# Convolution weights' zeros and bands issued by SyncE instead of GpSimd

## The chip, the cores and the metric

The kernel runs on one core of one Trainium2 chip. The metric is the device time of one execution in microseconds (us); the kernel before has a median of 3051.75 us over three runs (3051.0 to 3055.79). The core has five engines that run side by side, each through its own list of instructions: TensorE (PE, matrix products), VectorE (DVE), ScalarE (ACT), GpSimd (POOL) and SyncE (SP). SP, ACT and POOL issue DMA transfers. All transfers run on the same 16 DMA engines of the core, but each issuing engine has its own queue there.

## The reference

Two layers work on an image x of shape (2, 256, 64, 64) in float32. The first is attention over all 4096 pixels of an image with 8 heads, mixed with x by a mask. The second is a channel gate, attention in windows of 8 x 8 pixels, and two grouped 7 x 7 convolutions (64 groups of 4 channels), whose result gates x.

```python
# layer 0
m = jax.image.resize(mask, (B, 1, H, W), method='bilinear')
q, k, v = proj(Wq, bq) / math.sqrt(hd), proj(Wk, bk), proj(Wv, bv)
attn = jax.nn.softmax(jnp.einsum('bnd,bmd->bnm', q, k), axis=-1)
fuse = jnp.einsum('bnm,bmd->bnd', attn, v)
hybrid = _conv1x1(jnp.concatenate([x, fuse], axis=1), Wf, bf)
x = hybrid * m + x * (1.0 - m)
# layer 1
x = x * sigmoid(relu(xp @ ca_w1 + ca_b1) @ ca_w2 + ca_b2)
x = x + window_attention(x) @ out_w + out_b
x = channel_shuffle(x, 4)
y = lax.conv_general_dilated(x, sa_w1, (1, 1), [(3, 3), (3, 3)], feature_group_count=cr)
y = relu(_bn(y + sa_b1))
y = lax.conv_general_dilated(y, sa_w2, (1, 1), [(3, 3), (3, 3)], feature_group_count=cr)
y = _bn(y + sa_b2)
return x * jax.nn.sigmoid(y)
```

## The kernel before

A first part (to about 187 us) projects x to q, k and v and stores them to scratch tensors in HBM. Beside it, `prepare` (L166) builds from the convolutions' parameters two small tables `r1_s` and `r2_s` and a block of zeros `zero_s`, all in HBM; its DMAs go through POOL, ending with L303, L324 and L327. The stores of v (L484) go through POOL too.

`pipeline` (L523) does the attention of the first layer in 1024 slots. A slot is one image, one chunk of 512 queries, one group of four heads and one block of 128 keys. PE computes the scores (L632) two slots ahead, ACT the exponentials (L642) into one of eight buffers e, PE the products with v (L661), and DVE adds the exponentials up for the denominators (L663). Every four slots need one piece of k and one of v, 256 KB each. `load_piece` (L552) issues both on SP two pieces ahead; there are three buffers for each, so a load waits until PE is through with the piece that lay in its buffer. SP also loads q (L566), x and the mask (L572, L575).

The rest of the two layers for a finished chunk (`stage`, L720) is mixed into later slots; it starts a few slots after the chunk's last one, so the first 64 slots and some more have none of it. At the end of a stage the chunk's result goes to the scratch `x_s` by DMAs on POOL (L978). Slots run in the order written here; nothing reorders the instructions of an engine.

The convolutions at the end (`convolve`, L991) read their weights as banded matrices from the scratch `w_s` (16 blocks, one for each `u`), with `load_w` (L1006, SP). `bands` (L337) writes these blocks. It is a generator that issues one DMA at each step: 16 copies of `zero_s` into the 16 blocks (L341, 896 KB each), and then 156 bands: 28 rows of `r1_s` (L349), 112 rows of `r2_s` (L355) and 16 shift rows (L362), each spread along a diagonal of all 16 blocks in pieces of 112 or 28 bytes. The loop over slots takes one step when the slot's number leaves 1 on division by five (L1188), and drains what is left before it starts the convolutions' first loads at slot 960 (L1170):

```python
            if i % 5 == 1:
                next(banded, None)
            if i % 4 == 0:
                run_stages()
```

A step puts the DMA into its engine's list at that place of the program. When it is issued depends on what that engine waits for. On POOL there is little else in these slots: the stores of `x_s` at the end of a stage, later a few stores of the output.

Of the kernel before, what the change touches and what calls it, by code (L numbers as in the profile page):

```python
# [55 lines left out]
def conv_seq_kernel(ctx: ExitStack, tc: tile.TileContext, a, out):  # L56
    nc = tc.nc
# [68 lines left out]
    w_s = dram.tile([NU, P, 2 * 32 * UW], F32, name="ws")  # L126
# [33 lines left out]
    zero_s = dram.tile([P, 2 * 32 * UW], F32, name="zeros")  # L160
# [171 lines left out]
    def spread(row, n):  # L332
        f = row.shape[-1]
        return row.rearrange("p u f -> u p f").to_broadcast([NU, n, f])


    def bands():  # L337
        band1 = w_s.rearrange("u p (m f) -> u (p m) f", f=UW)
        band2 = w_s.rearrange("u p (m f) -> u (p m) f", f=UW // 4)
        for u in range(NU):  # L340
            nc.gpsimd.dma_start(w_s[u], zero_s)  # L341
            yield
        for q in range(4):
            for dy in range(KS):
                r0, r1 = max(0, dy - PAD), min(RB, RB + dy - PAD)
                p0, m0, n = 32 * q + 1 + r0, 1 + r0 - dy + PAD, r1 - r0
                k = KS * q + dy
                at0, step = p0 * 64 + m0, 64 + 1
                nc.gpsimd.dma_start(  # L349
                    band1[:, at0 : at0 + step * (n - 1) + 1 : step, :], spread(r1_s[k : k + 1], n)  # L350
                )
                yield
                for i in range(4):
                    at0, step = p0 * 256 + 128 + i * 32 + m0, 256 + 1
                    nc.gpsimd.dma_start(  # L355
                        band2[:, at0 : at0 + step * (n - 1) + 1 : step, :],
                        spread(r2_s[k : k + 1, :, i], n),
                    )
                    yield
            for i in range(4):  # L360
                at0 = 32 * q * 256 + 128 + i * 32 + 1
                nc.gpsimd.dma_start(  # L362
                    band2[:, at0 : at0 + RB, :], spread(r2_s[32 + q : 33 + q, :, i], RB)
                )
                yield
# [157 lines left out]
    def pipeline(arm, shifted, pools):  # L523
# [628 lines left out]
        def run_stages():  # L1152
            while stages:
# [3 lines left out]
                stages.popleft()  # L1157

        banded = bands()

        nc.scalar.activation(warm, ones[0:1, 0:1], AF.Exp)
# [132 lines left out]
```

## Time and profile before

| what | us |
|---|---|
| median of three runs | 3051.75 |
| the profiled execution | 3062.01 |
| its span | 3060.2 |
| PE busy | 2967.3 |
| DVE busy | 2498.5 |
| ACT busy | 2478.7 |
| POOL busy | 369.4 |
| first scores of the attention start | 187.1 |
| last scores end, about | 2823 |

A busy time counts an engine's own work; the rest of the span it waits. What it waited for stands in brackets in the order of time and in the list of waits. The profile calls SP's issuing of DMAs SPq, and says for a group of DMAs on POOL how long they took from issue to landing. In names such as `ka<-ks` the target stands first: `ka` is the piece of k in the core's memory, `ks` its scratch in HBM, `ws` the weights' scratch, `zeros`, `r1s` and `r2s` what it is filled from.

### The profile page before, as it was taken

Reading aid. Unit: us, or ns where it says so; the run is one execution under the profiler, and the core shown is the slowest. Engines: PE = TensorE matmul, PEld = TensorE weight load, DVE = VectorE, ACT = ScalarE, POOL = GpSimd, SP = SyncE. Lnnn points to the kernel's source line nnn. Section 1 sums busy time; section 2 is a strip of 40 time slices with the busy share of each in tenths; the row PEclk is TensorE's granted clock in tenths of the full one; section 3 lists DMA queues with packets and bytes.
Section 4 is the critical chain, followed back from the end, with each engine's and each line's share of the span. In section 5 each row is a group of like instructions: output and inputs, shape, how many; then the busy total and the mean of one; then the engine's idle time right before and its main releaser. Section 6 shows DMA issues by size and latency. Waiting matters only on the chain.

```text
span 3060.2 us, 60785 instructions
## 1 busy us (share of the span) xinstructions
PE 2967.3 (97%) x25114; PEld 1005.6 (33%) x25114; DVE 2498.5 (82%) x1347; ACT 2478.7 (81%) x4147; POOL 369.4 (12%) x636
## 2 busy tenths in 40 slices
PE   9968989999999999999999999999999999999897
PEld 3541222222322222232222232322222322223675
DVE  3227989899989999899999898999999898999211
ACT  5537969898989899898989898989898898988333
POOL 8020000101010101010100101010101000000256
PEclk9988999999999999999999999999999999999999
DMA  8574212424252424243322314242424232423364
GB/s 241 200 248 106 63 52 60 71 63 73 60 78 60 70 70 73 67 66 75 63 65 64 68 60 73 62 71 60 69 71 71 66 71 66 102 63 101 96 208 112
DMA packets 155999, 266.02 MB, mean 87 GB/s; under 512 B 43016, under 2 KB 61756, under 8 KB 155456
## 3 DMA queue, kind: packets, MB, share of 16 engines
q1 hardware_dynamic: 127424, 213.86, 25.3%
q0 software_dynamic: 23728, 45.48, 9.8%
q8 instruction: 200, 3.28, 0.5%
q10 hardware_dynamic: 4560, 2.70, 0.3%
q14 instruction: 87, 0.71, 0.1%
HBM read 213.49 MB, written 66.13 MB: 91 GB/s over the span
## 4 chain that ended last, share of the span: by engine, by line
PE 71%; DVE 13%; DMA 4%; issue 2%; ACT 2%; POOL 1%; SPq 0%; DVEq 0%; ACTq 0%
PE sa L632 29%; PE ava L661 27%; DVE suma L663 11%; PE qka L802 4%; PE hya L731 4%; DMA ka<-ks 2%; PE vwa L888 2%; ACT ea L642 1%; PE opa L952 1%; PE c2a L1067 1%; POOL out_dram L1102 1%; DMA wa<-ws 1%; PE c1a L1043 1%; PE sca L836 1%; PE rda L699 1%
## 5 line engine op out<-in xcount | busy, mean ns | idle before, releaser
L663 DVE TENSOR_TENSOR suma<-suma,ea 128x2048 f32<-128x2048 f32 x960 | 2198.7, 2290 | 122.7 <-ACT ea L642 39.5
L642 ACT ACTIVATE ea<-sa 128x512 f32<-128x512 f32 (+1 forms) x3072 | 2043.7, 745 | 122.0 <-PE sa L632 75.4
L632 PE MATMUL sa<-qa,ka 32*128 32x512 f32 x8192 | 1186.6, 641 | 39.7 <-DMA ka<-ks 38.2
L661 PE MATMUL ava<-ea,va 128*32 128x512 f32 x8192 | 1093.8, 605 | 0.3 <-ACT fa L671 0.3
L632 PEld LDWEIGHTS sa<-qa,ka 32*128 32x128 f32 x8192 | 331.2, 183 | 793.6 <-ACT ea L642 688.7
L661 PEld LDWEIGHTS ava<-ea,va 128*32 128x32 f32 x8192 | 161.8, 108 | 781.9 <-issue 755.7
L978 POOL DMA_DIRECT2D xs<-xo x94 | 66.1, 711 | 2302.4 <-DVE xo L963 2302.2
L1102 POOL DMA_DIRECT2D out_dram<-za x204 | 114.9, 571 | 102.4 <-DVE za L1089 55.5
L802 PE MATMUL qka<-ua,qkv_w 128*128 128x512 f32 x256 | 118.4, 605 | 0.0
L663 DVE TENSOR_TENSOR suma<-ea,ea 128x2048 f32<-128x2048 f32 x32 | 73.1, 2285 | 51.3 <-ACT ea L642 51.3
L1089 DVE TENSOR_TENSOR za<-za,xla 128x1536 f32<-128x1536 f32 (+1 forms) x16 | 22.6, 1409 | 110.0 <-ACT za L1083 56.7
L453 DVE TENSOR_REDUCE top<-sq 128x512 f32<-128x2048 f32 x16 | 36.6, 2286 | 81.4 <-ACT sq L447 81.4
L739 ACT ACTIVATE ta<-hya,bf 128x512 f32<-128x512 f32 x32 | 20.3, 684 | 99.7 <-PE hya L731 99.7
L1067 PE MATMUL c2a<-yca,wa 32*128 32x192 f32 (+1 forms) x1288 | 95.9, 440 | 4.0 <-issue 3.8
L1077 ACT ACTIVATE za<-c2a 128x384 f32<-128x384 f32 (+1 forms) x46 | 25.8, 615 | 86.3 <-DMA out_dram<-za 50.2
L743 DVE TENSOR_TENSOR ta<-ta,mca 128x512 f32<-128x512 f32 x32 | 22.0, 689 | 88.3 <-ACT ta L739 88.3
L1067 PEld LDWEIGHTS c2a<-yca,wa 32*128 32x128 f32 x1288 | 87.0, 314 | 14.9 <-issue 14.0
L857 ACT ACTIVATE ewa<-ewa,mxwa 128x64 f32<-128x64 f32 x256 | 85.5, 362 | 1.5 <-DVE mxwa L848 1.5
L355 POOL DMA_DIRECT2D ws<-r2s x112 | 69.7, 625 | 95.3 <-DMA ws<-r2s 48.6
L815 ACT ACTIVATE qka<-qka,qkv_b 128x512 f32<-128x512 f32 x64 | 40.7, 695 | 41.6 <-PE qka L802 41.6
L802 PEld LDWEIGHTS qka<-ua,qkv_w 128*128 128x128 f32 x256 | 46.0, 189 | 71.3 <-issue 58.7
L434 PE MATMUL q<-x,WqT 128*128 128x512 f32 x128 | 62.2, 631 | 5.6 <-DMA WqT<-in_WqT_dram 5.6
(141 smaller groups left out, 1620.5 us busy)
## 6 DMA issues: line engine op xcount, KB each, us to landing
ka<-ks SPq DMA_DIRECT2D x256, 256.0 KB
va<-vs SPq DMA_DIRECT2D x256, 256.0 KB
wa<-ws SPq DMA_DIRECT2D x17, 896.0 KB
ws<-zeros POOLq DMA_DIRECT2D x16, 896.0 KB, 23.9
xs<-xo POOLq DMA_DIRECT2D x78, 140.0 KB, 8.0
xla<-xs SPq DMA_DIRECT2D x25, 420.0 KB
x<-in_x_dram SPq DMA_DIRECT2D x16, 512.0 KB
qs<-qst SPq DMA_DIRECT2D x16, 512.0 KB
```

The source lines that it names most:

```text
L355: nc.gpsimd.dma_start(band2[:, at0 : at0 + step * (n - 1) + 1 : step, :], spread(r2_s[k : k + 1, :, i], n),)
L434: nc.tensor.matmul(s[:, g, :], w[:, kc, g * P : (g + 1) * P], rhs, start=(kc == 0), stop=(kc == KC - 1),)
L632: nc.tensor.matmul(heads[j], k[r, cols], q[r, g, :], start=True, stop=not shifted)
L642: nc.scalar.activation(e[:, h, :], tile, AF.Exp, scale=SCALE0)
L661: nc.tensor.matmul(av[r, :], v[:, m % PB, r], e[:, j, :], start=start, stop=stop)
L663: nc.vector.tensor_add(total, first[0] if m == 1 else total, e)
L731: nc.tensor.matmul(s[:, oc, :], wf[:, kc, oc * P : (oc + 1) * P], f[:, kc - KC, :] if half else xw[kc], start=(kc == 0), stop=(kc == 2 * K ...
L802: nc.tensor.matmul(s[:, j, :], wqkv[:, kc, o : o + P], u[:, kc, :], start=(kc == 0), stop=(kc == KC - 1),)
L857: nc.scalar.activation(e[:, n, :], e[:, n, :], AF.Exp, bias=mx[:, n : n + 1], accum_out=rs[:, n : n + 1],)
L978: eng.dma_start(x_s[b, n, p + r0 : p + r1].rearrange("r g w -> g r w"), xo[64 * h : 64 * h + 64, oc, r0 - WS * c : r1 - WS * c, :],)
L1067: nc.tensor.matmul(tiles[j // 2][:, j % 2, 0 : n * W], w[r, d], y[r, 0:n, d : d + W], start=(d == 0), stop=(d == KS - 1),)
L1102: engines[stores % len(engines)].dma_start(dst[b, i, r0:r1, UG * u : UG * u + UG, :], z[p + r0 : p + r1, :, nb * m + n, :],)
```

## The change

The four DMA issues in `bands` move from POOL to SP. The transfers, their order among themselves and the places in the program stay as they are. In SP's list they now stand between the loads of k and v: after the pair that the loop has issued last, and before the next. An empty line added above shifts all later line numbers by one.

```diff
     def bands():
         band1 = w_s.rearrange("u p (m f) -> u (p m) f", f=UW)
         band2 = w_s.rearrange("u p (m f) -> u (p m) f", f=UW // 4)
         for u in range(NU):
-            nc.gpsimd.dma_start(w_s[u], zero_s)
+            nc.sync.dma_start(w_s[u], zero_s)
             yield
         for q in range(4):
             for dy in range(KS):
...
-                nc.gpsimd.dma_start(
+                nc.sync.dma_start(
                     band1[:, at0 : at0 + step * (n - 1) + 1 : step, :], spread(r1_s[k : k + 1], n)
                 )
                 yield
                 for i in range(4):
                     at0, step = p0 * 256 + 128 + i * 32 + m0, 256 + 1
-                    nc.gpsimd.dma_start(
+                    nc.sync.dma_start(
                         band2[:, at0 : at0 + step * (n - 1) + 1 : step, :],
                         spread(r2_s[k : k + 1, :, i], n),
                     )
                     yield
             for i in range(4):
                 at0 = 32 * q * 256 + 128 + i * 32 + 1
-                nc.gpsimd.dma_start(
+                nc.sync.dma_start(
                     band2[:, at0 : at0 + RB, :], spread(r2_s[32 + q : 33 + q, :, i], RB)
                 )
                 yield
```

The waits in SP's list that come with it: each of these DMAs waits, as every DMA of SP does, for the landing of the one eight before it, and the first band waits for the last zeros as well. Between the third and fourth pieces the list reads:

```
k piece 2
v piece 2
ws <- zeros
k piece 3   (waits for PE)
v piece 3   (waits for PE)
ws <- zeros
k piece 4   (waits for PE)
```

## The prediction

> **What bounds the kernel now.** I read the page first, then PE's waits, then the order in time around the one long wait, engine by engine.
>
> ```profile
> span 3060.2 us, 60785 instructions
> PE 2967.3 (97%) x25114; PEld 1005.6 (33%) x25114; DVE 2498.5 (82%) x1347; ACT 2478.7 (81%) x4147; POOL 369.4 (12%) x636
> PE 71%; DVE 13%; DMA 4%; issue 2%; ACT 2%; POOL 1%; SPq 0%; DVEq 0%; ACTq 0%
> ws<-zeros POOLq DMA_DIRECT2D x16, 896.0 KB, 23.9
> ```
>
> TensorE is busy for 97% of the span, so a change that touches only DMA issue can win only what PE loses by waiting. The list of PE's waits has one large entry:
>
> ```profile
> PE sa L632 <- DMA ka<-ks: 38.2, 2, 37.7
> PE rda L699 <- issue: 9.0, 1, 9.0
> ```
>
> One wait of 37.7 us for a load of k. In PE's order of time:
>
> ```profile
> 202.32 1.06 PE L661 MATMUL ava<-ea,va 128*32 128x512 f32 x8
> 241.08 2.09 PE L632 MATMUL sa<-qa,ka 32*128 32x512 f32 x8 [37.69 <-DMA ka<-ks]
> 243.10 1.94 PE L661 MATMUL ava<-ea,va 128*32 128x512 f32 x8
> ```
>
> The load was issued on SP at 192.12 and is 48.82 us late in the chain of waits; the median k load lands 2.7 us after its issue (by the trace's landing records).
>
> ```profile
> 192.12 48.82 DMA ka<-ks
> ```
>
> What else ran is seen in POOL's order of time:
>
> ```profile
> 189.56 3.40 POOL L341 DMA_DIRECT2D ws<-zeros  x7 [0.19 <-issue]
> ...
> 216.09 0.49 POOL L341 DMA_DIRECT2D ws<-zeros  x1 [2.87 <-DMA ws<-zeros]
> 241.22 0.65 POOL L349 DMA_DIRECT2D ws<-r1s  x1 [24.64 <-DMA ws<-zeros]
> ```
>
> In the program the zeros stand five slots apart, but nothing on POOL holds them to that: they depend on no slot, so all 16 leave between 188.8 and 216.1 and land by about 241. That is 14 MiB read and written while PE needs the third piece of k. The windows show the DMA engines full and PE empty, against an ordinary stretch below:
>
> ```profile
> 203.40:241.10 37.70, 0.02 (x4) 0.05 (x4) 5.51 (x3) 1.01 (x2) 2.44 (x5) 0.54 0.96 312
> 300.00:355.00 55.00, 55.00 (x428) 12.54 (x432) 52.36 (x24) 53.37 (x81) 0.00 (x0) 1.00 0.27 73
> ```
>
> (Columns: length, busy time of PE, PEld, DVE, ACT, POOL, granted clock, DMA share, GB/s.) VectorE in the same stretch:
>
> ```profile
> 194.85 14.27 DVE L663 TENSOR_TENSOR suma<-suma,ea 128x2048 f32<-128x2048 f32 x6
> 245.19 2.29 DVE L663 TENSOR_TENSOR suma<-suma,ea 128x2048 f32<-128x2048 f32 x1 [36.07 <-ACT ea L642]
> 249.10 52.61 DVE L663 TENSOR_TENSOR suma<-suma,ea 128x2048 f32<-128x2048 f32 x22 [1.62 <-ACT ea L642]
> ```
>
> After 249.10 DVE runs without a gap above 0.5 us until the reciprocal at 397.45, for which PE waits its 9.0 us. An add comes every 2.39 us (52.61/22); PE needs 2.07 us for a slot there. So the first stretch, which has no window attention yet, is DVE's, and DVE's idle time decides what the wait costs.
>
> **What the Trainium skill says.** "DMA: Bandwidth & Descriptors", section Queues, rings and completion order: a DMA engine takes its queues in turn, a packet at a time. The trace agrees exactly: a zero transfer is 16 packets of 57,344 bytes (one per engine, median 2.75 us), k's packets are 2048 bytes (0.084 us when alone); between 196 and 236 us the packet records hold 424 packets of POOL's queue and 418 of SP's. Each small packet of k thus pays for a large one of zeros. The packets are far larger than the page's usual ones. The same page, section Anatomy of one DMA: DMA engines don't wait on semaphores, the issuing sequencer does. The 24.64 us on POOL before L349 agree. Its Specifications say that pieces under 512 bytes are read, modified and written; the bands' pieces have 28 or 112 bytes. The trace gives the price for POOL's path: the first band alone landed in 3.3 us, and the first nine, issued from 241.22, had all landed by 255.9, so 14.7/9 = 1.6 us each.
>
> **The change part by part.** Program order on SP becomes: k, v, then at every fifth slot one zero or band. The loads of k and v wait for their buffers (PE), so whatever stands behind them is now paced, which it was not on POOL.
>
> *Removed: the burst of zeros.* Around the wait SP will issue x at 191.1, the mask, k and v of the third piece (192.1, 192.6), then one zero, then k of the fourth. In one ring these run in order: 16 + 8 + 8 packets of 0.084 us end with k about 2.7 us after the ring starts, so k lands near 196; PE wants it at 203.4. The 37.69 us go. PE also ran its first groups afterwards at a lower clock (0.83 in 241 to 260): 2.09, 1.94, 2.09 and 1.22 us where 1.14, 1.06, 1.14 and 1.06 are usual, 2.9 us more. By PE alone the gain is 40.6. But DVE is late next: its 70 adds from 192.45 to the reciprocal need 70 x 2.39 = 167.3 us, so the reciprocal comes at 359.8 at the earliest, for 397.45 now: 37.7 us, which is also its idle time, 36.07 + 1.62. PE's wait of 9.0 us there remains. I take 37.7.
>
> *Added: 16 zeros on SP's ring.* One occupies each engine for 2.1 (the fastest 5% of those packets) to 3.3 us (the slowest 5%); I take 2.75. The k or v behind it is that much later. By the landing and start records, a k load has landed 18.3 us before its first use in the median and 14.8 in the lower quartile, so this is covered: cost 0. (The load with least left by then that isn't beside a burst of POOL is at 2660, behind the convolutions' first loads; no zero or band is near it.) Per zero (five slots; 31 adds of 2.39 in 32 slots make 11.6 us) the ring carries 2.75 + 1.25 x 16 x 0.084 = 4.4 us. Uncovered, each would cost its 2.75 us, 44 in all.
>
> *Added: 156 bands on SP's ring* (28 + 112 + 16). No trace shows them on SP, nor any transfer from HBM to HBM there. Lower bound 0.5 us (30 pieces at 18 ns, the time of SP's 256-byte output packets); nearest row 1.6 us; upper bound 3.5 us, POOL's first r2 band, which includes POOL's own generation. I take 1.6, covered by the same 14.8 us. Uncovered: 156 x 1.6 = 250 us; that is why the slack matters.
>
> *Added: SP's issue time.* 172 x 0.33 to 0.46 us (its other loads) = 57 to 79 us over 2200 us in which SP mostly waits for PE (1178 us for v alone): 0. *Added waits:* each SP transfer waits for the one eight before it, and the first band also for the last zero. Behind a waiting band stand k and v and the loads of q and x, and PE behind these. Eight transfers are some 2.8 pieces, over 22 us; landings of about 3 to 8 us are over by then: 0.
>
> *Moved past POOL:* the stores of x to its scratch (L978) no longer stand among bands, and POOL's bursts go. Today k loads near such bursts land after 12 to 21 us, and one costs PE 0.5 us (at 1872). Gain 0 to 0.5; I take 0. The last band goes at slot 856, about 2390 us, before the weights' first load at 2660: no cost at the tail.
>
> Sum: -37.7 us. The profiled execution took 3062.0 us (span 3060.2 and 1.8 around it), so the changed one 3024.3. It stands 10.3 us above the median 3051.75; whether part of that excess lies in the burst is not shown, so the gain without a profile may be 28 to 38. Taken in full: 3014.
>
> **Rivals.** (a) *The gain is given back by the zeros.* If SP's path copies HBM to HBM slowly, a zero overloads the ring once it takes more than 11.6 - 1.7 = 9.9 us; 16 x 1 us at 11 us gives 3030. For: a zero's median landing now is 23.3 us. Against: eight were in flight then, 2.9 us each. (b) *The wait is not the zeros' doing*, or moves to the same place by another cause, such as the mask's broadcast ahead of k: 3052. Against: the even count of packets, and the mask's and k's packets at 1891 took mostly 0.084 us. (c) *Slower: bands clog SP's ring.* In steady work five slots take 12.9 us ((2822 - 187)/1024 x 5), of which k, v, q, x and mask take about 2. A band above 10.9 us holds k back every time; from 11.2 us the gain is used up (156 x 0.24 = 38). At 12 us: 156 x 1.1 = 172 less 38, so 3186. For: tiny pieces to HBM, ahead of k in one ring, with no other queue to run beside. Against: 1.6 us measured, and 30 pieces would need 0.37 us apiece.
>
> **How the numbers follow.** Forecast 0.86 (its own range 3008 to 3024: from a full gain with the small extras, 43, to 28), (a) 0.07, (b) 0.02, (c) 0.05. Since (a) to (c) hold 0.14, the range only widens a little towards (a): 3007 to 3026. A difference under 0.2%, 6 us, can't be told from none. Faster: 0.86 + 0.07 = 0.93; same 0.02; slower 0.05.
>
> **What would show it.** Right: PE's wait for ka gone from its list; DVE's adds unbroken from 192.45 to a reciprocal near 360; zeros on SP one per five slots; DMA share near 0.4 instead of 0.96 at 203 to 241; k landings after POOL's bursts below 10 us. Wrong: a wait of PE for ka or va anywhere between slots 8 and 856, repeated every fifth slot for (c), within the first 80 slots for (a); or SP's issues of bands lasting several us.

## The result, and the profile after

The changed kernel takes 3015.18 us in the median (3014.3 to 3020.05, four runs), the kernel before 3053.71 beside it: 38.5 us less, a ratio of 0.9878 with a 95% interval of 0.986 to 0.9895. A second set of runs gave 0.9865 (0.9849 to 0.988), 40.9 us below 3062.45. One of twelve runs of a later kernel (bands alone, below) took 4161.77 us at a granted clock of 0.65 and is left out of its ratio.

The profiled execution took 3014.3 us. In its list of PE's waits (total, times, longest) the load of k is gone, and the one for the reciprocal is there as before:

```profile
span 3012.4 us, 60778 instructions
...
PE rda L700 <- issue: 9.0, 1, 9.0
PE rda L700 <- DVE inva L714: 8.9, 12, 0.7
PE q L435 <- DMA WqT<-in_WqT_dram: 5.6, 1, 5.6
PE nrm L415 <- DVE top L454: 3.0, 2, 2.1
PE c1a L1044 <- DMA xla<-xs: 2.3, 1, 2.3
```

SP's order of time shows why. A zero follows a pair of loads, and the next loads wait for PE, so the 16 zeros are strung out from 193.5 to 369.4 us. The first two of them:

```profile
192.65 0.35 SPq L560 DMA_DIRECT2D ka<-ks  x1
193.06 0.42 SPq L562 DMA_DIRECT2D va<-vs  x1
193.53 0.60 SPq L342 DMA_DIRECT2D ws<-zeros  x1
194.42 0.34 SPq L560 DMA_DIRECT2D ka<-ks  x1
199.50 0.32 SPq L562 DMA_DIRECT2D va<-vs  x1
199.87 0.89 SPq L342 DMA_DIRECT2D ws<-zeros  x1
```

The windows of the same two stretches as in the prediction. PE (second figure) is busy all through the first, and the DMA engines (second from the end) are at 0.44 instead of 0.96. The second now holds some of the zeros, and at its end the start of PE's wait for the reciprocal:

```profile
203.40:241.10 37.70, 37.70 (x296) 8.77 (x296) 36.04 (x17) 36.53 (x55) 0.00 (x0) 1.00 0.44 141
300.00:355.00 55.00, 51.92 (x408) 16.72 (x408) 52.71 (x24) 44.81 (x69) 0.00 (x0) 1.00 0.38 124
```

And DVE's order of time, from its first add to the reciprocal:

```profile
192.63 2.29 DVE L664 TENSOR_TENSOR suma<-ea,ea 128x2048 f32<-128x2048 f32 x1 [51.32 <-SPq L1291]
195.03 69.38 DVE L664 TENSOR_TENSOR suma<-suma,ea 128x2048 f32<-128x2048 f32 x29
264.87 2.29 DVE L664 TENSOR_TENSOR suma<-suma,ea 128x2048 f32<-128x2048 f32 x1 [0.46 <-ACT ea L643]
...
360.14 0.95 DVE L714 RECIPROCAL inva<-inva 128x128 f32<-128x128 f32 x1
```

No gap above 0.5 us is left. The reciprocal comes at 360.14 where it came at 397.45: 37.3 us, nearly the whole gain, are won at this point, before any stage has begun.

The two spans differ by more, 47.8 us. Followed by pieces of k, the lead is 37.3 us at the reciprocal and 39.7 where the scores of piece 242 start (2677.5 against 2637.8); the other 8.1 us lie after it, in the convolutions. The experiments below show where the 2.4 us in between come from, and that the last part is not the change's.

### The profile page after: what moved, and what is told of

It reads as the page before. It is cut to its first block, busy times and chain, and to the rows that moved or that the text cites. A ratio compares the mean times of both kernels' runs of the same rounds, so it can differ in the third digit from the quotient of the medians.

```text
span 3012.4 us, 60778 instructions
## 1 busy us (share of the span) xinstructions
PE 2959.5 (98%) x25114; PEld 1003.8 (33%) x25114; DVE 2498.8 (83%) x1347; ACT 2479.0 (82%) x4147; POOL 263.7 (9%) x464
## 4 chain that ended last, share of the span: by engine, by line
PE 73%; DVE 18%; issue 3%; ACT 2%; DMA 2%; POOL 1%; SPq 0%; DVEq 0%; ACTq 0%; POOLq 0%
PE sa L633 28%; PE ava L662 25%; DVE suma L664 16%; PE qka L803 4%; PE hya L732 4%; PE vwa L889 2%; PE v L472 2%; PE q L435 2%; PE k L435 2%; POOL out_dram L1103 1%; ACT ea L643 1%; DMA out_dram<-za 1%; DVE za L1090 1%; PE c2a L1068 1%; PE sca L837 1%
## 5 line engine op out<-in xcount | busy, mean ns | idle before, releaser
L1068 PEld LDWEIGHTS c2a<-yca,wa 32*128 32x128 f32 x1288 | 86.9, 314 | 12.7 <-issue 11.5
L1044 PE MATMUL c1a<-xla,wa 128*32 128x384 f32 (+1 forms) x896 | 61.1, 421 | 2.3 <-DMA xla<-xs 2.3
```

What stands on the lines that cost most here:

```text
L1044: nc.tensor.matmul(s[32 * j : 32 * j + 32, 0 : n * W], w[:, j, d, :], xs[k][:, 0:n, j, d : d + W], start=(d == 0), stop=(d == KS - 1),)
L1068: nc.tensor.matmul(tiles[j // 2][:, j % 2, 0 : n * W], w[r, d], y[r, 0:n, d : d + W], start=(d == 0), stop=(d == KS - 1),)
```

## The experiments

**Which part of the change wins.** Three kernels: the one before again, only the zeros moved, only the bands moved.

```diff
# e0_before: no edit
# e1_zeros_sp, against the kernel before
-            nc.gpsimd.dma_start(w_s[u], zero_s)
+            nc.sync.dma_start(w_s[u], zero_s)
# e2_bands_sp, against the changed kernel
-            nc.sync.dma_start(w_s[u], zero_s)
+            nc.gpsimd.dma_start(w_s[u], zero_s)
```

> The kernel before, profiled a second time, to see which of its parts repeat. Theory (the 38 us are the one wait behind the zeros): again one wait of PE for ka of 36 to 39 us between 203 and 242, the reciprocal of the first chunk at 396 to 399, and the rest of the profile as before within some us. The profiled execution of before was 10 us above the median of its runs; if that excess was chance in the tail (after the last scores), the span from the k load at 2660 to the end is here some 391 us as after the change, and not 400. Rival (the change also shortens the tail): 398 to 402 again.

> Only the 16 zeros move to SP, the 156 bands stay on POOL. Theory (zeros alone make the wait): the whole gain, 36 to 39 us below before; no wait of PE for ka over 1 us at 203. Rival (the bands' bursts on POOL hold loads back too and carry part of the gain): 5 to 20 us less gain, with waits for ka or va near POOL's bursts.

> Only the 156 bands move to SP, the 16 zeros stay on POOL. Theory: no change, within 3 us of before; the wait of about 38 us for ka stands at 203 as before. The first band then waits on SP for the last zeros, but it comes some 200 us after they have landed. Rival (bands' bursts matter): a gain of 5 us or more.

Measured: the kernel before again 3057.86 us (one run; 3056.81 the median of before beside it); zeros alone 3020.8, ratio 0.9879 (0.9862 to 0.9895); bands alone 3056.97, ratio 0.9994 (0.9985 to 1.0003). The window 203.4 to 241.1 of the three, in this order:

```profile
203.40:241.10 37.70, 0.09 (x4) 0.00 (x0) 5.61 (x3) 1.11 (x2) 2.43 (x5) 0.53 0.96 312
```

```profile
203.40:241.10 37.70, 37.70 (x298) 8.71 (x296) 36.04 (x17) 36.52 (x56) 0.00 (x0) 1.00 0.41 137
```

```profile
203.40:241.10 37.70, 0.44 (x6) 0.00 (x0) 5.96 (x3) 1.46 (x3) 2.43 (x5) 0.53 0.94 317
```

The zeros carry nearly the whole gain: with the bands alone PE is as empty as before, with the zeros alone it is full. In the times of whole runs no gain of the bands can be told (0.9994, with 1 inside the interval), but the profiles show a small one. The 2.4 us by which the kernel before falls back further, after the reciprocal, are lost at three places (1.0, 0.8 and 0.9 us, at pieces 35, 68 and 163; elsewhere it gains 0.3 us in small amounts), each with 12 or 13 bands issued by POOL in the 40 us before. In e0 most of the loss is one wait of PE in the midst of a slot, right beside a band; `issue` stands for a wait whose cause the profile doesn't show:

```profile
893.92 0.61 POOL L355 DMA_DIRECT2D ws<-r2s  x1 [2.15 <-DMA ws<-r1s]
894.54 1.05 PE L661 MATMUL ava<-ea,va 128*32 128x512 f32 x3 [1.70 <-issue]
```

Measured in the same way against the changed kernel, from piece 26 to 242, all five profiles with the bands on POOL lose time (before 2.4 us, before again 2.3, zeros alone 1.4, and 4.9 and 7.5 in e3 and e7 below), and those with the bands on SP none (within 0.2 us: bands alone, e4, e5 and the changed kernel again). So in the profiles some 1.4 to 2.4 us of the gain are the bands'. How they hold PE up is open.

The tail settles with the same runs. From piece 242 to the end the profiles have 382.7 us (before), 378.9 (before again), 380.1 (zeros alone), 382.2 (bands alone), 374.6 (changed) and 381.8 (changed again, below). The changed kernel stands at the low end once and near the high end once, so the 8.1 us between the first profiles of the two kernels are chance between executions. The expectation for e0, 391 us "from the k load at 2660", counted from the load's issue and had its after-value from the one short tail; counted so, e0 has about 396, between its two cases.

**Pacing, or only another queue.** All 16 zeros on SP at once, ahead of the third piece (e4):

```diff
+        for _ in range(NU):
+            next(banded)
         for i in range(2):
             scores(i)()
```

> Zeros and bands on SP as in the change, but all 16 zeros are issued at once, after the first loads and ahead of k of the third piece, instead of one every fifth slot. Theory (the pacing by the loads of k and v is what wins, not SP's queue as such): k of the third piece stands behind 16 zeros of 2.75 us in one ring, so it lands near 195 + 44 = 239 and PE waits 33 to 40 us for ka at 203; within 5 us of before. Rival (moving off POOL's queue is enough): no wait over 10 us, and 30 us or more gained.

Measured: 3059.93 us (one run) beside 3058.88 for before. SP's order of time and PE's wait:

```profile
193.09 27.33 SPq L342 DMA_DIRECT2D ws<-zeros  x16
222.70 0.33 SPq L560 DMA_DIRECT2D ka<-ks  x1
225.69 0.33 SPq L562 DMA_DIRECT2D va<-vs  x1
```

```profile
243.28 2.09 PE L633 MATMUL sa<-qa,ka 32*128 32x512 f32 x8 [39.45 <-DMA ka<-ks]
```

On the same queue without the pacing nothing is won. Here the load is not outrun by other packets: it stands behind the zeros, first on SP, whose transfers wait for the landing of the one eight before, so that k is issued only at 222.70, and then in SP's ring (its queue on a DMA engine). What wins is that the loads, which wait for PE, stand between the zeros. Whether zeros paced in the same way on POOL's queue would do as well was not tried.

**Why a load of 256 KB took 48.8 us: turns by packet, or bytes that must pass first.** Both put the wait at the same place in the kernel before, since k landed just as the zeros ended. Two kernels leave the burst on POOL and make its packets smaller.

```diff
# e3_small_pool: pieces of 448 floats, read from one row
+            nc.gpsimd.dma_start(
+                w_s[u].rearrange("p (m f) -> (p m) f", f=448),
+                zero_s[0:1, 0:448].to_broadcast([4 * P, 448]),
+            )
# e7_rows_pool: rows of 1792 floats, source and target in different orders
+            nc.gpsimd.dma_start(
+                w_s[u].rearrange("(b a) f -> b a f", b=16),
+                zero_s.rearrange("(a b) f -> b a f", b=16),
+            )
```

> The zeros stay on POOL in one burst, with the same bytes to write, but each as 512 pieces of 1792 bytes, all read from one row of zeros, so that a packet is at most a few KB and not 56 KB. Theory (a queue's turn is a packet, so k's 2 KB packets each paid for 56 KB of zeros): the 32 packets of SP's ring up to k then wait for some 0.2 us each, k of the third piece lands near 202 and the wait for ka falls to between 0 and 8 us; 28 to 38 us faster than before. Rival (the 14 MiB have to pass before k, whatever the packets): a wait of 30 us or more remains, and at most 8 us are gained.

> The zeros stay on POOL in one burst and read and write the same bytes as in the kernel before, but source and target are walked in different orders, so that a packet is one row of 7168 bytes instead of 57,344. Theory (the queues take turns by packets): a zero packet takes some 0.34 us (an eighth of 2.75), so the 35 packets of SP's ring up to k of the third piece need 35 x 0.43 = 15 us from about 196 on; k lands near 212 while zeros run on to 240, PE waits 5 to 14 us at 203, and the kernel is 22 to 34 us faster than before. Rival (k waits until the bytes of the zeros have passed): a wait of 30 us or more and at most 8 us gained. It repeats the question of the run with pieces of 1792 bytes, whose zeros took 9 us each and not 2.8.

The first missed: 3079.38 us, ratio 1.007 (1.0052 to 1.0087), slower than before. Its wait for ka at 203 is 28.7 us, and shorter ones follow at the later pieces:

```profile
232.31 2.09 PE L635 MATMUL sa<-qa,ka 32*128 32x512 f32 x8 [28.68 <-DMA ka<-ks]
```

Its windows:

```profile
203.40:241.10 37.70, 9.03 (x56) 2.06 (x56) 9.15 (x5) 6.33 (x10) 2.50 (x4) 0.59 1.00 142
260.00:300.00 40.00, 28.53 (x192) 5.88 (x184) 27.50 (x12) 24.02 (x36) 0.62 (x1) 0.88 0.98 140
```

The DMA engines are full at 140 GB/s instead of 312: written in this way the zeros leave POOL every 9 us instead of every 2.9, and last to about 338, when the first band goes. Nearly all of its packets had 5376 bytes, and these took 0.70 us in the median, not the 0.2 expected. With that figure the theory's own sum gives 35 x (0.70 + 0.08) = 27 us from 204.1, when the first packet of SP starts, so 231; PE went on at 232. That this first packet starts only 12.7 us after its load was issued (4.6 us in the kernel before, 1.0 in the changed one) is not explained by turns; its cause stays open. The rival is contradicted too, as k came about 100 us before the zeros were through. But this run changed two things at once, the size of the packets and the speed of the zeros.

The second separates them. Its zeros last about as long as in the kernel before (the first band goes at 247.65, before at 241.22), its packets have 7168 bytes and took 0.27 us in the median, and PE's waits are

```profile
PE rda L702 <- issue: 9.0, 1, 9.0
PE rda L702 <- DVE inva L716: 7.4, 10, 0.7
PE sa L635 <- DMA ka<-ks: 7.1, 1, 7.1
```

```profile
203.40:241.10 37.70, 30.59 (x232) 6.99 (x232) 30.72 (x14) 28.12 (x43) 2.65 (x6) 0.91 0.99 359
```

The wait for ka is 7.1 us instead of 37.7, with the DMA engines just as full (0.99) and the same bytes of zeros to write: 3030.37 us, ratio 0.9894 (0.9878 to 0.991), 32 us below before. k lands at 210.4, expected was 212. So it is the size of the competitor's packets that starved the load. The packet records count the turns: from 206 to 216 us 451 packets of POOL's queue and 447 of SP's here, 100 and 100 in the kernel before.

**What the bands cost on SP.** Each band issued twice, the second time into scratch that nothing reads (e5; shown for one of the three kinds of band):

```diff
+    w2_s = dram.tile([NU, P, 2 * 32 * UW], F32, name="w2s")
...
                 nc.sync.dma_start(
                     band1[:, at0 : at0 + step * (n - 1) + 1 : step, :], spread(r1_s[k : k + 1], n)
                 )
+                nc.sync.dma_start(
+                    band1b[:, at0 : at0 + step * (n - 1) + 1 : step, :], spread(r1_s[k : k + 1], n)
+                )
...
```

> The change, with every band issued twice on SP, the second time into a scratch tensor that nothing reads: 156 more transfers of the disputed kind ahead of the loads of k and v. Theory (a band takes 1 to 2 us of the ring and the loads have 10 us or more left): within 3 us of the changed kernel, so 35 to 40 us below before, with no wait of PE for ka or va. Rival (the bands are near the limit of what SP's ring carries): 156 x 1.6 us = 250 us slower than the changed kernel if nothing covers them, or some tens of us where they collide with the loads of x and the mask.

Measured: 3017.74 us, ratio 0.9863 (0.9848 to 0.9878), against 0.9878 and 0.9865 for the changed kernel: no cost. PE has no wait for ka or va. The stretch 900 to 1800, in the changed kernel, in its second profile (e8) and here:

```profile
900.00:1800.00 900.00, 895.94 (x7604) 262.05 (x7600) 834.23 (x426) 804.29 (x1374) 22.54 (x32) 1.00 0.26 67
```

```profile
900.00:1800.00 900.00, 895.99 (x7608) 262.05 (x7600) 834.32 (x425) 804.24 (x1375) 22.54 (x32) 1.00 0.28 67
```

```profile
900.00:1800.00 900.00, 896.02 (x7604) 261.95 (x7604) 834.15 (x426) 804.21 (x1375) 22.54 (x32) 1.00 0.31 69
```

The DMA share rises from 0.26 or 0.28 to 0.31 with 70 more bands. As two profiles of one kernel differ by 0.02 themselves, the packets tell more: those of the 70 bands in the changed kernel's stretch take 19.1 us of all 16 engines together, 0.27 us for a band.

**What is late next.** The changed kernel, and the same with the first chunk's reciprocal spread five slots later, first alone (e6), then both on one chip (e8, the changed kernel, and e9):

```diff
+                lag = 5 if (b, c) == (0, 0) else 0
-                at(DN + 2, lambda: spread(0))
-                at(DN + 3, lambda: spread(1))
+                at(DN + 2 + lag, lambda: spread(0))
+                at(DN + 3 + lag, lambda: spread(1))
...
-                at(DN + 5, lambda b=b, c=c: stages.append(stage(b, c)))
+                at(DN + 5 + lag, lambda b=b, c=c: stages.append(stage(b, c)))
```

> The change, and for the first chunk alone the two products that spread the reciprocal (L700) and all that follows on them five slots later; the reciprocal stays where it is. It tests that DVE sets the first stretch. Theory: PE's wait of 9.0 us for the reciprocal, which comes six adds late on DVE, goes, since five slots lie between; as PE goes on at DVE's pace of 2.39 us a slot instead of 2.07, only part of it is won: 2 to 9 us below the changed kernel. Rival (PE loses the same time a little later, because DVE's backlog stays): within 1.5 us of the changed kernel.

> The changed kernel again, on the chip of the run below, for its tail and as the measure for that run. Theory: 36 to 41 us below before; no wait of PE for ka; reciprocal at 360; the stretch from the use of piece 242 to the end between 374 and 383 us as in all profiles so far, so that the tail owes nothing to the change.

> The version that spreads the first chunk's reciprocal five slots later, again, beside the changed kernel on one chip. Theory: 3 to 9 us below the changed kernel (its first profile shows the 9.0 us wait gone). Rival (the lower time of the first run was the chip's or chance): within 2 us of it.

Measured: e6 3010.92 us, ratio 0.9843 (0.983 to 0.9857). Together: the changed kernel 3021.53 (0.9865, 0.9849 to 0.988), the later spread 3011.25 (0.9834, 0.982 to 0.9847); their runs don't overlap (3020.06 to 3022.02 and 3010.24 to 3013.56). The wait is gone:

```profile
PE rda L700 <- DVE inva L714: 8.1, 11, 0.7
PE q L435 <- DMA WqT<-in_WqT_dram: 5.7, 1, 5.7
PE c1a L1048 <- DMA xla<-xs: 4.1, 1, 4.1
...
PE hya L736 <- DVE fa L720: 1.5, 1, 1.5
PE qka L807 <- DVE ua L797: 1.4, 1, 1.4
```

The later spread is 10.3 us faster, all of the 9.0 and a little over, where at most 9 were expected (in the profiles 9.6 at piece 242): the reciprocal stays at 359.9, but PE goes on past it with slots of 2.07 us. DVE's backlog, which held PE to 2.4 us a slot up to 345, costs it after that only two waits of some 1.5 us, in the stage's first products and at 413. This kernel beats both others, 51 us below the one before.

## Why the prediction was right

It said 3014 us, and 3015.2 was measured. That the two figures meet within 1.2 us is in part luck: the two medians of the kernel before are 2 us apart, and the bands' small gain was put at nothing. The gain is the better measure: 37.7 us forecast, 38.5 and, in the second set of runs (e8), 40.9 measured.

- *The burst and its wait*: right. e1 and e2 give the zeros the whole of this wait, e4 says that SP's queue without the pacing leaves it.
- *Turns by packet*: right, shown by e7. Two things were too simple. Not every packet of k paid for a large one: half of POOL's packets in that stretch are 4-byte completions (49 of 100 from 206 to 216 us), so every second one did. And the agreement is not exact from the start: SP's first packet came 4.6 us after its load's issue, which turns don't explain.
- *DVE caps the gain, 37.7 and not the 40.6 of PE alone*: right in place and size. The reciprocal was put at 359.8 and came at 360.14; the 9.0 us wait remained, as said. In e7 it shows once more: PE's wait there is 7.1 us, DVE's idle time 5.49 and 0.35, and the reciprocal comes 5.5 us later than in the changed kernel.
- *k of the third piece near 196*: too early. By the landing records it landed 6.0 us after its issue, at 198.7, with 4.8 us left and not 7. The first 512 packets of SP's ring, 32 for each engine, took 0.135 us in the mean and not 0.084: 4.3 us instead of 2.7. The rest lies around the packets and was left out of the sum; what it is made of is not shown.
- *Zeros at 2.75 us each*: 2.47 us in the median on SP's queue; hidden, as said.
- *Bands at 1.6 us*: over-sized; 0.27 us of the engines by their packets, and 3.0 us from issue to landing in the median. Rival (c), which needed 10.9 us, falls with it.
- *SP's issue time, 57 to 79 us*: by the medians 16 x 0.47 + 156 x 0.54 = 92 us, somewhat more and as well hidden.
- *POOL's bursts gone from beside k*: the slowest hundredth of k's loads landed after 8.4 us or more instead of 30. The gain was put at 0 to 0.5 us and taken as 0; in the profiles it is 2.4 us, of which only 0.5 us was a wait for k.
- *10.3 us of profile above the median, perhaps part of the burst*: no sign of it. The median of the runs won all of the 38. Where that excess lay is not shown; the tail alone varies by 8 us from one execution to the next.

## What to carry to other kernels

The 16 zeros depended on nothing and left POOL within 27 us (188.8 to 216.1), though the program spaces them over 75 slots. So look in the trace for when a DMA really goes, and put it behind instructions that wait if it has to be paced. Beside a queue of large packets, a load of small packets was slowed here by the size of the others' packets, not by their share of bytes: smaller packets (e7, 32.1 us) won most of what the pacing won on the same chip (e8, 40.9 us). What a removed wait is worth is set by the next engine in line: DVE's idle time in it (37.7 us, where PE lost 40.6) foretold the 37.3 us won at the reciprocal.

## What the hardware showed that was not expected

The two kinds of queue cut the same transfers differently. The page's lines for SP's queue (q1) and POOL's (q0), before and after (packets, MB, share of 16 engines):

```profile
q1 hardware_dynamic: 127424, 213.86, 25.3%
q0 software_dynamic: 23728, 45.48, 9.8%
```

```profile
q1 hardware_dynamic: 201472, 231.60, 26.6%
q0 software_dynamic: 18224, 27.73, 4.2%
```

POOL's queue lost 5504 packets, which is 172 x 32: for each of the 172 transfers one data packet and one completion for each of 16 engines, 27 to 30 pieces of a band in one packet. SP's gained 74,048: every piece of 28 or 112 bytes is a packet there. In spite of that a band on SP's queue lands after 3.0 us in the median. POOL's bands, which go in bursts, took 11.4 in the median, but the very first, with nothing in flight before it, 3.3; so the two queues may hardly differ for a band on its own.

Writing zeros in pieces of 1792 bytes all read from one row (e3) ran at 140 GB/s on full engines, in rows of 7168 bytes from 128 rows (e7) at 359, loads of k and v included. Whether the single source row or the smaller piece is to blame was not tried.
